# Norms spread through memory, an earlier second chunk, and two reordered steps in an attention and expert kernel

## The chip, the cores and the metric

The kernel runs on one core of one Trainium2 chip. Its engines are TensorE (PE; its weight loads are shown apart as PEld), VectorE (DVE), ScalarE (ACT), GpSimd (POOL) and SyncE (SP), which here only issues transfers. The metric is device time in microseconds (us) for one execution. Three runs of the kernel before took 1643.99, 1644.94 and 1645.40 us.

## The reference, cut to what matters

Four images `x[4, 32, 128, 128]` pass through a channel attention and then through a token layer. Of the first layer:

```
xs = x.reshape(B, C, h, R, w, R).transpose(0, 1, 3, 5, 2, 4).reshape(B, C * R * R, h, w)   # R = 2
q = xs.reshape(B, C * R * R, hw)                     # 128 channels, 64 x 64 = 4096 positions
energy = einsum('bci,bcj->bij', q, q)                # positions against positions
d = sqrt(diagonal(energy, axis1=1, axis2=2))
attn = softmax(energy / (d[:, :, None] * d[:, None, :]), axis=-1)
out = gamma * einsum('bcj,bij->bci', q, attn).reshape(B, C * R * R, h, w) + xs
```

So each position's vector of 128 channels is divided by its own norm `d` before the products. The energy is symmetric, and so are its exponentials; only the row sums make the softmax.

The second layer reads each image as 4096 tokens of 128 values (32 channels of 128 rows each, a row being a token; 32 groups of 128 tokens): a layer norm and a linear attention without softmax (`K^T V`, 8 heads), added to the tokens; then a layer norm, a router over 8 experts, the best two of them with weights that add to one, the experts' products, and the weighted sum added to the tokens. All is float32.

## The kernel before, in words

**Attention.** An image's 4096 positions are cut into 8 chunks of 512, read in four pairs (`kc` 0 to 3). For each chunk the kernel holds `qT` (positions on partitions) and `qn` (channels on partitions, divided by the norm). `attend` walks the lower triangle: for row `i` and tile `jc <= i` it takes four steps `j`. A step emits a product `pe` of `qn` with `qn` (L609), its exponential on ACT with the row sum, `pr` (L612), and, through `after`, things due some steps later: the product `values` into the one bank `po` (L497) two steps later, and for tiles off the diagonal a DVE transpose of `pr` into `F` (L421). When a row is done ACT empties `po` into `o` (L502). Once four steps of a tile are in `F`, SP stores it to memory (L530) and loads it back with its groups swapped (L545), and `transposed_share` multiplies it with `qT` (`pg`, L433) for the mirrored tile; the diagonal has `diagonal_share` (L453).

**Pacing.** The order on PE, DVE, ACT and SP is the order in which the program emits (`manual_schedule`); POOL is pinned where needed. `clock` counts the steps' work: a step adds 8 units (less on the diagonal), a share 4. A share is emitted by `step_share` when its due value, 57 units after its loads, is reached. The side work (preparing chunks, loading weights, the second layer) is written as generators. A table `timed` gives each a window in per cent of the image and a number of moves; a move advances it twice, once before a step and once after. The second layer's parts move every 10 units.

**Preparing a pair of chunks.** `prep` loads `xa` (`load_quarters`, L308), turns it by DVE to `qT` (`turn_quarters`, L316), squares and sums it (L295, L296), and raises the sums to the power -1/2 on POOL (L164), into `rn`, one value per position with positions on partitions. `qn` needs these values along the free axis. So DVE widens `rn` (`wide`, L388), PE transposes `wide` in four pieces into the bank `pnorm` (L399), and DVE multiplies the rows with it (L372). `prep_first` treats image 0's first pair in another way: it scales `qT` by `rn` (L338) and PE transposes the result (`ptn`, L344). At the program's start `prep_first` and the second pair's `prep` are advanced by hand, before the loop. `xa` lies in the pool `xin` with one buffer.

**Second layer.** `close_rows` divides and adds. `attention_rows(u)` takes eight groups of 128 tokens: three times a product `pat` (L855), whose sum `add_rows` puts into the tokens `T`; then eight statistics (`batch_stats`, L962), the router's first sums (`router_rows`), and `close_stats`, six small DVE operations after which POOL makes `rsf`, `nbf` and `nbo`. `normalise` (L696) on ACT uses these. Several `u` run staggered.

What the walk through a row emits in one step, before:

```
after(2, partial(values, pr[:, c0:], t, c0, CH))
...
turn_tick()
clock[0] += 2 * (CH - c0) // P
step_share()
yield
```

Of the kernel before, what the change touches and what calls it, by code (L numbers as in the profile page):

```python
# [22 lines left out]
def kernel(  # L23
# [258 lines left out]
    def chunks_of(b, kc, st):  # L282
        qT = qpool.tile([P, 2, NJ, P], F32, tag="qT", name=f"qT_{b}_{kc}")
        st.setdefault("qT", {})[2 * kc] = qT[:, 0]
        st["qT"][2 * kc + 1] = qT[:, 1]
        return qT
# [12 lines left out]
        rows = st["T"][:, ts(kc, 8), :]  # L299
        return rows.rearrange("p k (w r) -> p k w r", r=2)  # L300

    def load_quarters(b, kc, queues=(nc.sync, nc.sync)):

        xa = xin.tile([P, 2, 2, 2, HW2, 2], F32, tag="xx", name=f"xa_{b}_{kc}")
        halves = x[b].rearrange("c (s g) w -> c s (g w)", s=2)
        for a in (0, 2, 1, 3):
            first_row = 16 * kc + 4 * a
            queues[a // 2].dma_start(  # L308
                xa[ts(a, S)].rearrange("p s k r w e -> p s (k r w e)"),
                halves[:, :, first_row * W : (first_row + 4) * W],  # L310
            )
        return xa

    def turn_quarters(s, xa, qT):
        for k in range(2):
            nc.vector.transpose(  # L316
                qT[:, s, 2 * k : 2 * k + 2, :].rearrange("p h (e r c) -> p r (h e) c", e=2, r=2),
                xa[:, s, k].rearrange("p r (h t) e -> p (r h) e t", h=2),
            )

    def prep_first(st):

        b, kc = 0, 0
        st["T"] = big1.tile([P, KT, D], F32, tag="T", name="T_0")
        xa = load_quarters(b, kc, (nc.sync, nc.scalar))
        qT = chunks_of(b, kc, st)
        yield
        ss = stat.tile([P, 2 * NJ], F32, tag="ss", name=f"ss_{b}_{kc}")
        rn = stat.tile([P, 2 * NJ, 1], F32, tag="rn", name=f"rn_{b}_{kc}")
        for s in range(2):  # L330
            turn_quarters(s, xa, qT)
            squares(b, kc, s, qT, ss)
            pow_neg_half(rn[:, ts(s, NJ), 0], ss[:, ts(s, NJ)])
        keep_running(40, ps_g, "pg")
        scaled = []
        for s in range(2):
            qs = work.tile([P, NJ, P], F32, tag="qs", name=f"qs_{b}_{kc}_{s}", bufs=2)
            nc.vector.tensor_tensor(qs, qT[:, s], rn[:, ts(s, NJ)].to_broadcast([P, NJ, P]), ALU.mult)  # L338
            scaled.append(qs)
        for s, qs in enumerate(scaled):  # L340
            qn = channels(b, kc, s, st)
            pt, done = hold(f"ptn_{b}_{kc}_{s}", lambda p, qn=qn: nc.scalar.activation(qn, p, AF.Copy))  # L342
            for j in range(NJ):
                nc.tensor.transpose(pt[:, ts(j, P)], qs[:, j, :], ident)  # L344
            done()
            yield

    def prep(b, kc, st):

        ahead = 2 if b == 0 and kc == 1 else 5
        xa = load_quarters(b, kc)
# [3 lines left out]
        for _ in range(ahead):  # L357
            yield
        qT = chunks_of(b, kc, st)
        for s in range(2):  # L360
# [17 lines left out]
        rn = stat.tile([P, 2 * NJ, 1], F32, tag="rn", name=f"rn_{b}_{kc}")  # L378
        for s in range(2):
            squares(b, kc, s, qT, ss)  # L380
            if s == 1:
                pow_neg_half(rn[:, :, 0], ss)
            yield
        for _ in range(ahead - 2):
            yield
        wide = work.tile([P, NJ, 2, 64], F32, tag="qs", name=f"wide_{b}_{kc}", bufs=2)
        for s in range(2):
            nc.vector.tensor_copy(wide[:, :, s], rn[:, ts(s, NJ)].to_broadcast([P, NJ, 64]))  # L388
        yield
        if b:  # L390
            yield

        def scale_all(bank):
            for s in range(2):
                scale(s, bank, lambda ap: ap.rearrange("p (j a t) -> p a j t", a=4, t=S))

        bank, done = hold(f"pnorm_{b}_{kc}", scale_all)
        for j in range(NJ):
            nc.tensor.transpose(bank[:, ts(j, P)], wide[:, j].rearrange("p s c -> p (s c)"), ident)  # L399
        yield  # L400
        done()
        yield
# [7 lines left out]

    BELOW = {1: 0, 2: 1, 3: 3}

    def after(ticks, f):
        queued.append((tick[0] + ticks, f))

    def turn_tick():

        due = [f for at, f in queued if at <= tick[0]]
        queued[:] = [q for q in queued if q[0] > tick[0]]
        for f in due:  # L420
            f()  # L421

    def in_order(ap):
        return ap.rearrange("p (a j c) -> p j a c", a=4, c=S)
# [49 lines left out]
    def attend(b, st):  # L474
# [11 lines left out]
        for i in range(NCH):  # L486
# [94 lines left out]
            for jc in order:  # L581
# [21 lines left out]
                for j in range(NJ):  # L603
# [10 lines left out]
                    own.append(pr)  # L614
                    if ending and jc == order[-1] and j == NJ - 1:
                        st["exps"] = True
                    after(2, partial(values, pr[:, c0:], t, c0, CH))
                    if jc < i and not both:
                        after(1, partial(nc.vector.transpose, Fb[:, :, :, j, :], pr))
                        if j == NJ - 1:  # L620
# [33 lines left out]
    def layer1(b, st):  # L654
# [288 lines left out]
        def attention_rows(u):  # L943

            if u < 3:
                fetch_blocks(u + 1)
            yield
            for g in (2 * u, 2 * u + 1):
                keep[g] = work.tile([P, CH], F32, tag="grp", name=f"xnT_{b}_{g}", bufs=2)
                nc.vector.transpose(keep[g], keep["blocks", u][:, ts(g % 2, 4), :].rearrange("p k d -> p (k d)"))  # L950
                yield
            yield
            la = stat.tile([P, 8, 2 * E], F32, tag="la", name=f"la_{b}_{u}")
            for j0 in range(0, 8, 3):
# [12 lines left out]
            close_stats("f", 8 * u, 8, bs)  # L967
            next(logits)
            yield
            nc.sync.dma_start(t2[:, ts(u, 8)], T[:, ts(u, 8), :])  # L970
            yield
            for g in (2 * u, 2 * u + 1):
                normalise(range(4 * g, 4 * g + 4), rsf, nbo)
                if g % 2:
                    for _ in logits:
                        pass
                yield
                yield
            if u % 2:
                for _ in route(u // 2):  # L980
# [4 lines that stand above are left out]
                yield from sorted_experts(u // 2)  # L985
# [510 lines left out]
    for b in range(B):  # L1496

        if b == 0:
# [80 lines left out]
```

## Time and profile before

One execution was profiled.

| | |
|---|---|
| median of three runs | 1644.94 us |
| the profiled execution | 1638.94 us |
| its span | 1637.1 us |
| granted PE clock, mean | 0.996 |
| instructions | 20938 |
| memory read, written | 166.90 MB, 182.09 MB |
| `pr` exponentials on ACT (L612) | 576, mean 560 ns |
| `po` products (L497) | 1152 records, mean 559 ns |
| `pe` products (L609, 128x512 of two chunks) | 896 records, mean 596 ns |
| `pg` products (L433) | 880 records, mean 593 ns |
| `F` transposes (L421) | 440, mean 700 ns |
| POOL's power for a chunk pair (L164, 128x8) | 15, mean 1660 ns |

How to read it: an f32 product shows as two records on PE. The records' durations overlap, because products are pipelined; the distance between starts tells what a product costs. The profile counts as idle what lies between the end of one record and the start of the next, and names who released the waiting instruction. A granted clock below 1 means that PE ran at a part of its speed in that stretch. Along the chain of waits PE has 84% of the span, with L497 25%, L609 24% and L433 21%.

### The profile page before, as it was taken

To read this page: it belongs to the slowest core of one execution; us is meant where nothing else is said; L and a number is where in the kernel's file an instruction comes from. 1 tells how busy PE (TensorE), PEld (TensorE's weight loads), DVE (VectorE), ACT (ScalarE), POOL (GpSimd) and SP (SyncE) were. 2 spreads that over 40 slices of the span, in tenths; PEclk is the share of its full clock that TensorE was granted. 3 is DMA by queue.
4 is the path that set the end of the run, shared out by engine and by line. 5 is a ranking of instruction groups with operands and counts; after the bars stand their busy time and mean duration, and the time that the engine had idled before them with its cause. 6 is when DMAs were issued, how large, how long until landed. Compare 5 with 4: busy or idle time off the path is not lost.

```text
span 1637.1 us, 20938 instructions
## 1 busy us (share of the span) xinstructions
PE 1598.4 (98%) x5075; PEld 832.8 (51%) x5075; DVE 942.7 (58%) x2383; ACT 877.2 (54%) x2779; POOL 593.8 (36%) x565
## 2 busy tenths in 40 slices
PE   8999999999999999999999999999999999999887
PEld 5444444455554455555554445555554445555633
DVE  5444353468487454449468545447758644344786
ACT  3555445456465544546555554556646554555386
POOL 1000000001024442446545553156555653437166
PEclk9999999999999999999999999999999999999999
DMA  4555656675759798997898889798798989886001
GB/s 139 199 193 174 202 179 213 236 231 179 171 206 269 238 230 248 255 263 206 208 221 270 263 214 277 216 281 222 203 212 256 298 238 257 252 254 192 15 14 39
DMA packets 364728, 345.18 MB, mean 211 GB/s; under 512 B 157504, under 2 KB 291136, under 8 KB 350272
## 3 DMA queue, kind: packets, MB, share of 16 engines
q1 hardware_dynamic: 330144, 304.33, 62.1%
q0 software_dynamic: 26624, 25.58, 7.7%
q10 hardware_dynamic: 7840, 13.93, 2.9%
q8 instruction: 43, 0.70, 0.2%
q14 instruction: 77, 0.63, 0.1%
HBM read 166.90 MB, written 182.09 MB: 213 GB/s over the span
## 4 chain that ended last, share of the span: by engine, by line
PE 84%; DVE 6%; DMA 4%; ACT 2%; issue 1%; POOL 1%; SPq 1%; ACTq 0%; DVEq 0%; POOLq 0%
PE po L497 25%; PE pe L609 24%; PE pg L433 21%; PE py L1371 3%; PE pg L453 2%; DMA F<-blocks 2%; PE pys L1180 2%; PE pys L1130 2%; PE pgram L725 2%; PE pat L855 1%; SPq L545 1%; DMA below<-F 1%; PE pys L1137 1%; ACT xn L696 1%; ACT pr L612 1%
## 5 line engine op out<-in xcount | busy, mean ns | idle before, releaser
L612 ACT ACTIVATE pr<-pe 128x512 f32<-128x512 f32 (+1 forms) x576 | 322.4, 560 | 614.5 <-PE pe L609 592.1
L497 PE MATMUL po<-pr,qT 128*128 128x512 f32 (+3 forms) x1152 | 549.8, 559 | 4.2 <-ACT o L502 3.5
L609 PE MATMUL pe<-qn,qn 128*128 128x512 f32 x896 | 460.4, 596 | 4.7 <-ACT pr L612 4.7
L433 PE MATMUL pg<-F,qT 128*128 128x512 f32 x880 | 450.4, 593 | 4.6 <-DMA F<-blocks 4.6
L421 DVE STREAM_TRANSPOSE F<-pr 128x512 f32<-128x512 f32 x440 | 305.1, 700 | 167.5 <-ACT pr L612 160.1
L497 PEld LDWEIGHTS po<-pr,qT 128*128 128x128 f32 x1152 | 215.6, 191 | 251.5 <-issue 219.4
L1245 POOL DMA_INDIRECT acc<-ys,place x128 | 202.1, 1579 | 210.4 <-ACT pr L612 135.0
L438 ACT ACTIVATE junk<-F 128x512 bf16<-128x512 f32 x440 | 273.1, 621 | 5.1 <-DMA F<-blocks 5.1
L433 PEld LDWEIGHTS pg<-F,qT 128*128 128x128 f32 x880 | 166.7, 190 | 199.5 <-issue 176.2
L1066 POOL DMA_INDIRECT xs<-xn,place x192 | 185.7, 967 | 176.3 <-ACT pr L612 109.8
L609 PEld LDWEIGHTS pe<-qn,qn 128*128 128x128 f32 x896 | 158.0, 191 | 131.4 <-issue 119.2
L442 DVE TENSOR_TENSOR o<-o,pg 128x512 f32<-128x512 f32 x110 | 75.2, 683 | 244.6 <-PE pg L433 244.4
L164 POOL TENSOR_TENSOR rn<-ss,neg_half 128x8 f32<-128x8 f32 (+1 forms) x17 | 27.2, 1603 | 321.0 <-DVE ss L296 320.9
L612 ACT ACTIVATION_READ_ACCUMULATOR pr<-pe 128x1 f32 x576 | 111.8, 194 | 0.0
L609 PE MATMUL pe<-qn 128*128 128x512 f32 (+3 forms) x256 | 91.5, 440 | 0.7 <-ACT qn L342 0.7
L1245 POOL DMA_INDIRECT yb<-ys,place x64 | 61.0, 953 | 77.8 <-DMA ys<-results 47.5
L438 ACT ACTIVATION_READ_ACCUMULATOR junk<-F 128x1 f32 x440 | 84.6, 192 | 0.0
L1112 DVE TENSOR_TENSOR results<-pys,xn 128x256 f32<-128x256 f32 (+1 forms) x60 | 24.9, 416 | 83.5 <-ACT xn L1106 70.4
L164 POOL TENSOR_TENSOR rsa<-dm_a,neg_half 128x8 f32<-128x8 f32 x16 | 28.9, 1807 | 104.7 <-DVE sv_a L688 104.6
L696 ACT ACTIVATE xn<-T,nbo,rsf 128x128 f32<-128x128 f32 x128 | 54.1, 495 | 20.7 <-POOL nbo L692 20.7
L1371 PE MATMUL py<-ew_sb,xn 128*128 128x512 f32 x128 | 60.2, 610 | 5.0 <-ACT tmp L1327 3.9
L164 POOL TENSOR_TENSOR rsf<-dm_f,neg_half 128x8 f32<-128x8 f32 (+1 forms) x15 | 26.3, 1751 | 105.2 <-DVE sv_f L688 105.2
(221 smaller groups left out, 1508.0 us busy)
## 6 DMA issues: line engine op xcount, KB each, us to landing
blocks<-F SPq DMA_DIRECT2D x110, 1024.0 KB
F<-blocks SPq DMA_DIRECT2D x220, 192.0 KB
F<-blocks SPq DMA_DIRECT2D x220, 128.0 KB
F<-blocks SPq DMA_DIRECT2D x220, 64.0 KB
below<-F SPq DMA_DIRECT2D x31, 384.0 KB
T<-in_x_dram SPq DMA_DIRECT2D x64, 128.0 KB
out_dram<-acc SPq DMA_DIRECT2D x128, 64.0 KB
xa<-in_x_dram SPq DMA_DIRECT2D x62, 128.0 KB
```

The source lines that it names most:

```text
L164: pinned(nc.gpsimd.tensor_tensor(dst, src, neg_half.to_broadcast(list(src.shape)), ALU.pow))
L421: f()
L433: nc.tensor.matmul(pg.rearrange("p (a f) -> p a f", a=4), st["qT"][i][:, ib, :], G[:, :, ib], start=(ib == 0), stop=(ib == NJ - 1),)
L438: nc.scalar.activation(junk, G[:, :, ib], AF.Copy, accum_out=st["sums"][:, NJ * i + ib, jc : jc + 1])
L442: nc.vector.tensor_tensor(st["o"][jc], st["o"][jc], pg, ALU.add)
L497: nc.tensor.matmul(row["po"][:, lo:hi], qT[blk // NJ][:, blk % NJ, :], w, start=start, stop=(row["left"] == 0))
L609: nc.tensor.matmul(pe[:, c0:], qn[jc][:, ts(j, P)], qn[i][:, c0:], start=True, stop=True)
L612: nc.scalar.activation(pr[:, c0:], pe[:, c0:], AF.Exp, accum_out=sums[:, t, i : i + 1]).ins
L696: nc.scalar.activation(xn[:, k, :D], T[:, k, :], AF.Identity, scale=rs[:, k, :], bias=nb[:, k, :])
L1066: inst = nc.gpsimd.indirect_dma_start(xs[h], offset(place[:, i, k : k + 1]), xn[:, k, :], None)
L1245: inst = nc.gpsimd.indirect_dma_start(to, None, ys, offset(place[:, i, k : k + 1]), compute_op=op)
L1371: nc.tensor.matmul(bank, xn[:, k, :D], ew_sb[:, 4 * h : 4 * h + 4, :], start=True, stop=True)
```

## The change

It has four parts.

1. **Norms.** For every pair except image 0's first two, POOL writes the power into one of two fixed tiles `norms` (128x32, of which 8 columns are used, the rest set to 1 at the start). DVE transposes the tile in blocks of 32, SP stores it (16 KB) to a memory tile, and two SP loads bring it back, each row repeated over 64 partitions, into `spread_...`. There are five yields after the store and five after the loads; then `scale` multiplies with that tile. `wide`, its two copies, the four transposes and the bank `pnorm` go, except for image 0's second pair.
2. **Image 0's start.** The second pair is loaded into another pool (`work`, tag `wide`) right after the first. Its four turns stand between the first pair's steps, whose order is now written by hand; its squares follow at once. Its generator then has 8 moves from 1.3 to 5.5% instead of 10 from 0.5%. The order by hand begins before `prep_first`'s work instead of after it.
3. **Statistics.** In `attention_rows` each sum is followed by the statistics of its two or three groups, and `close_stats` follows the last at once; the router's first sums come two yields after it.
4. **Share first.** At the third step of a row's first tile, the `values` that are due are emitted behind the share.

The tile `weight` has one buffer instead of two. The diff, cut to its core:

```diff
-    def load_quarters(b, kc, queues=(nc.sync, nc.sync)):
-        xa = xin.tile([P, 2, 2, 2, HW2, 2], F32, tag="xx", name=f"xa_{b}_{kc}")
+    def load_quarters(b, kc, queues=(nc.sync, nc.sync), place=(xin, "xx")):
+        xa = place[0].tile([P, 2, 2, 2, HW2, 2], F32, tag=place[1], name=f"xa_{b}_{kc}")
...
+    def turn_quarter(s, k, xa, qT):
+        nc.vector.transpose(
+            qT[:, s, 2 * k : 2 * k + 2, :].rearrange("p h (e r c) -> p r (h e) c", e=2, r=2),
+            xa[:, s, k].rearrange("p r (h t) e -> p (r h) e t", h=2),
+        )
...
+    norms = [const.tile([P, S], F32, tag=f"norm{n}", name=f"norm_{n}") for n in range(2)]
+    for norm in norms:
+        nc.gpsimd.memset(norm, 1.0)
...
     def prep_first(st):
...
+        scaled = []
+        keep_running(40, ps_g, "pg")
+        summed(0, rows_squared(0))
+        sq = rows_squared(1)
+        st["turns"].pop(0)()
+        scale_rows(0)
+        summed(1, sq)
+        st["turns"].pop(0)()
+        st["turns"].pop(0)()
+        scale_rows(1)
+        st["turns"].pop(0)()
...
+    def spread_over_rows(norm, nm, tag, spread, gap):
+        turned = stat.tile([P, S], F32, tag="turned", name=f"turned_{nm}", bufs=1)
+        nc.vector.transpose(turned, norm)
+        yield
+        kept = dram.tile([P, S], F32, tag="norms", name=f"norms_{nm}", bufs=3)
+        nc.sync.dma_start(kept, turned)
+        for _ in range(gap):
+            yield
+        wide = work.tile([P, CH], F32, tag=tag, name=f"spread_{nm}", bufs=2)
+        for s in range(2):
+            nc.sync.dma_start(
+                wide[ts(s, 64)].rearrange("p (a f) -> p a f", a=4),
+                kept.rearrange("(a q) t -> a (q t)", q=S)[:, ts(s, P)].partition_broadcast(64),
+            )
+        spread.append(wide)
+        for _ in range(gap):
+            yield
...
     def prep(b, kc, st):
...
+        if not on_chip:
+            yield from idle(1)
+            yield
+            spread = []
+            yield from spread_over_rows(norm, f"{b}_{kc}", "qs", spread, 5)
+            for s in range(2):
+                scale(s, spread[0], lambda ap: ap.rearrange("p (a j t) -> p a j t", a=4, t=S))
+            yield
+            return
...
-    def turn_tick():
-        due = [f for at, f in queued if at <= tick[0]]
+    def turn_tick(starts=False):
+        due = [q for q in queued if q[0] <= tick[0]]
         queued[:] = [q for q in queued if q[0] > tick[0]]
-        for f in due:
-            f()
+        for _, f, can_wait in due:
+            if not (starts and can_wait):
+                f()
+        return [f for _, f, can_wait in due if starts and can_wait]
...
-                    after(2, partial(values, pr[:, c0:], t, c0, CH))
+                    after(2, partial(values, pr[:, c0:], t, c0, CH), True)
...
-                    turn_tick()
+                    left = turn_tick(jc == order[0] and j == 2)
                     clock[0] += 2 * (CH - c0) // P
                     step_share()
+                    for f in left:
+                        f()
                     yield
...
-        weight = stat.tile([P, 2, KT, 1], F32, tag="weight", name=f"weight_{b}")
+        weight = stat.tile([P, 2, KT, 1], F32, tag="weight", name=f"weight_{b}", bufs=1)
...
                 attend_rows(u, j0, pa)
                 yield
                 done()
-            bs, stats = batch_stats("f", 8 * u, 8)
-            for j in range(8):
-                stats[j]()
-                if j == 3:
-                    yield
-                    yield
+                for f in stats[j0 : j0 + 3]:
+                    f()
+            close_stats("f", 8 * u, 8, bs)
+            yield
+            yield
             logits = router_rows(nc.vector, 8 * u, 8, la)
-            close_stats("f", 8 * u, 8, bs)
             next(logits)
-            yield
             nc.sync.dma_start(t2[:, ts(u, 8)], T[:, ts(u, 8), :])
+            yield
             yield
...
-    next(first)
-    load_weights()
+    ordered = ExitStack()
     next(first)
     next(second)
+    load_weights()
+    ordered.enter_context(tc.manual_schedule(engines=ENGINES))
+    next(second)
+    next(first)
     load_tokens(states[0]["T"][:, 0:8, :], 0, 0, 8)
-
-    ordered = ExitStack()
-    ordered.enter_context(tc.manual_schedule(engines=ENGINES))
-    timed = [(first, 0, 1, 2), (second, 0.5, 5.5, 10)]
+    next(second)
+    next(second)
+    timed = [(first, 0, 1, 2), (second, 1.3, 5.5, 8)]
```

In `prep_first`, `rows_squared(s)` is the two turns and the square of half `s`, `summed` its sum and the power, `scale_rows` its scaling (as before, into tag `grp`).

More of the change, by code (lines that the diff above doesn't have):

```diff
@@ L312, in load_quarters @@
         return xa
+    def turn_quarter(s, k, xa, qT):
[3 more added lines that the diff above has]
+        )
     def turn_quarters(s, xa, qT):
         for k in range(2):
[L316 to L319, printed above, removed]
+            turn_quarter(s, k, xa, qT)
+    norms = [const.tile([P, S], F32, tag=f"norm{n}", name=f"norm_{n}") for n in range(2)]
+    for norm in norms:
+        nc.gpsimd.memset(norm, 1.0)
     def prep_first(st):
@@ L328, in prep_first, with rows_squared, summed, scale_rows @@
         ss = stat.tile([P, 2 * NJ], F32, tag="ss", name=f"ss_{b}_{kc}")
-        rn = stat.tile([P, 2 * NJ, 1], F32, tag="rn", name=f"rn_{b}_{kc}")
-        for s in range(2):
+        rn = norms[0][:, : 2 * NJ][:, :, None]
+        def rows_squared(s):
             turn_quarters(s, xa, qT)
-            squares(b, kc, s, qT, ss)
+            sq = work.tile([P, NJ, P], F32, tag="qs", name=f"sq_{b}_{kc}_{s}", bufs=2)
+            nc.vector.tensor_tensor(sq, qT[:, s], qT[:, s], ALU.mult)
+            return sq
+        def summed(s, sq):
+            nc.vector.tensor_reduce(ss[:, ts(s, NJ)], sq, AX.X, ALU.add)
             pow_neg_half(rn[:, ts(s, NJ), 0], ss[:, ts(s, NJ)])
[L334 to L337, printed above, removed]
+        def scale_rows(s):
+            qs = work.tile([P, NJ, P], F32, tag="grp", name=f"qs_{b}_{kc}_{s}", bufs=2)
             nc.vector.tensor_tensor(qs, qT[:, s], rn[:, ts(s, NJ)].to_broadcast([P, NJ, P]), ALU.mult)
             scaled.append(qs)
+        scaled = []
[9 more added lines that the diff above has]
+        st["turns"].pop(0)()
         for s, qs in enumerate(scaled):
@@ L346, in prep_first @@
             yield
-    def prep(b, kc, st):
-        ahead = 2 if b == 0 and kc == 1 else 5
-        xa = load_quarters(b, kc)
+    def spread_over_rows(norm, nm, tag, spread, gap):
[15 more added lines that the diff above has]
+            yield
+    def prep(b, kc, st):
+        soon = b == 0 and kc == 1
+        ahead = 2 if soon else 5
+        if soon:
+            xa = load_quarters(b, kc, place=(work, "wide"))
+            yield
+        else:
+            xa = load_quarters(b, kc)
         if b == 0:
@@ L356, in prep @@
             xx = rows_of_image(b, kc, st)
-        for _ in range(ahead):
+        qT = chunks_of(b, kc, st)
+        if soon:
+            st["turns"] = [partial(turn_quarter, s, k, xa, qT) for s in range(2) for k in range(2)]
             yield
-        qT = chunks_of(b, kc, st)
-        for s in range(2):
+        for _ in range(0 if soon else ahead):
+            yield
+        for s in range(0 if soon else 2):
             turn_quarters(s, xa, qT)
@@ L377, in scale @@
                 )
-        rn = stat.tile([P, 2 * NJ, 1], F32, tag="rn", name=f"rn_{b}_{kc}")
+        on_chip = b == 0 and kc == 1
+        norm = norms[kc % 2]
         for s in range(2):
@@ L381, in prep @@
             if s == 1:
-                pow_neg_half(rn[:, :, 0], ss)
+                pow_neg_half(norm[:, : 2 * NJ], ss)
             yield
+        if not on_chip:
[7 more added lines that the diff above has]
+            return
+        rn = norm[:, : 2 * NJ][:, :, None]
         for _ in range(ahead - 2):
@@ L389, in prep @@
         yield
-        if b:
-            yield
+        yield
         def scale_all(bank):
@@ L411, with after @@
     BELOW = {1: 0, 2: 1, 3: 3}
-    def after(ticks, f):
-        queued.append((tick[0] + ticks, f))
-    def turn_tick():
-        due = [f for at, f in queued if at <= tick[0]]
+    def after(ticks, f, can_wait=False):
+        queued.append((tick[0] + ticks, f, can_wait))
+    def turn_tick(starts=False):
+        due = [q for q in queued if q[0] <= tick[0]]
         queued[:] = [q for q in queued if q[0] > tick[0]]
-        for f in due:
-            f()
+        for _, f, can_wait in due:
+            if not (starts and can_wait):
+                f()
+        return [f for _, f, can_wait in due if starts and can_wait]
     def in_order(ap):
@@ L953, in attention_rows @@
             la = stat.tile([P, 8, 2 * E], F32, tag="la", name=f"la_{b}_{u}")
+            bs, stats = batch_stats("f", 8 * u, 8)
             for j0 in range(0, 8, 3):
@@ L959, in attention_rows @@
                 done()
-            bs, stats = batch_stats("f", 8 * u, 8)
-            for j in range(8):
-                stats[j]()
-                if j == 3:
-                    yield
-                    yield
+                for f in stats[j0 : j0 + 3]:
+                    f()
+            close_stats("f", 8 * u, 8, bs)
+            yield
+            yield
             logits = router_rows(nc.vector, 8 * u, 8, la)
-            close_stats("f", 8 * u, 8, bs)
             next(logits)
+            nc.sync.dma_start(t2[:, ts(u, 8)], T[:, ts(u, 8), :])
             yield
-            nc.sync.dma_start(t2[:, ts(u, 8)], T[:, ts(u, 8), :])
             yield
```

## The prediction

> **What bounds the kernel now.** I read the page's first part, then TensorE's waits, then the timeline at each wait.
>
> ```profile
> PE 1598.4 (98%) x5075; PEld 832.8 (51%) x5075; DVE 942.7 (58%) x2383; ACT 877.2 (54%) x2779; POOL 593.8 (36%) x565
> ```
>
> TensorE (PE) is busy for all but 38.7 us of 1637.1. Every product taken off it, and every wait of its own, is time; work of the other engines counts only where it makes PE wait. Its waits (total, times, longest):
>
> ```profile
> PE pe L609 <- ACT pr L612: 4.7, 3, 1.6
> PE pg L433 <- DMA F<-blocks: 4.6, 3, 2.3
> PE po L497 <- ACT o L502: 3.5, 14, 0.5
> PE pnorm L399 <- DVE wide L388: 2.5, 2, 2.2
> PE ptn L344 <- DVE qs L338: 2.2, 1, 2.2
> ```
>
> Four of these five are touched; only the waits for F's transfer are not aimed at. In the timeline an f32 product is a pair (x2), and a 128x512 pair is followed by the next one 0.86 us later; that start-to-start time is the price used below, since the durations overlap.
>
> **Norms through DRAM.** Of 15 chunks that use the four `pnorm` transposes (60 in the tile's view), 14 lose them; only image 0's chunk 1 keeps them. The chain of waits, read in time order, has one such group:
>
> ```profile
> 60.16 0.22 PE po L497 x2
> 60.38 0.44 PE pnorm L399 x4
> 60.82 0.86 PE pe L609 x2
> ```
>
> It stands in a gapless PE: 14 x 0.44 = **6.2 us** gone. In exchange each chunk gets a 128x32 DVE transpose in place of two copies of 286 ns (the 128x256 transposes take 413, so no more than before), and SP gets three issues: a 16 KB store and two 128 KB loads, together 42 issues and 3.8 MB beside 345 MB. The scaling multiplies read SBUF where they read PSUM; 64x512 from PSUM took 686 ns, the 128x512 square from SBUF 667, so no change. They come some eight yields later; the tightest, chunk 3 of a later image (17 moves from 38 to 62%, scaled at the 12th: 53.5%), is still ahead of row 6, which starts at about 56%.
>
> A rule speaks against this part: the Trainium skill, "DMA: Bandwidth & Descriptors", section "Anatomy of one DMA", gives a DMA a fixed cost of about 2 us, mostly the receipt from the memory written. Two legs would be 4 us per chunk, 56 us if PE waited for them. This trace agrees on the size: `below` was stored from SP at 17.43 (0.35) and its loads went out at 19.78, 2.0 us later. But after the store the generator yields five times, and again after the loads; two yields are one move and a move is at least one step of 2.58 us (po starts 477.70, 480.28, 482.85), so each leg has 2.5 steps, over 6 us. I take 0. The other end: SP stands in order, and behind the store (which waits for DVE, which waits for POOL's power) stand the loads of F. These have room: issued by 35.69, first used at 46.18, so 10.5 us less the 2 us landing. Cover gone, each chunk costs what the F wait at 849 us cost: 2.3 idle and about 1.3 of slow clock, 3.6.
>
> **Image 0's start.** Now:
>
> ```profile
> 19.70 0.38 PE L497 MATMUL po<-pr,qT 128*128 128x128 f32 x2
> 22.32 1.07 PE L399 MATMUL pnorm<-ident,wide 128*128 128x128 f32 x4 [2.23 <-DVE wide L388]
> 23.18 1.92 PE L609 MATMUL pe<-qn,qn 128*128 128x512 f32 x2
> 24.89 1.49 PE L497 MATMUL po<-pr,qT 128*128 128x512 f32 x2
> 26.22 1.02 PE L609 MATMUL pe<-qn,qn 128*128 128x512 f32 x2
> ```
>
> PE could have gone on at 19.92 (19.70 and 0.22) and stood until 22.32: 2.40 lost. Then the group took 0.86 to the next start instead of 0.44, the next pair 1.71 instead of 0.86, the next 1.33 instead of 0.86: 1.74 more, at this clock (columns: stretch, length, busy of PE, PEld, DVE, ACT, POOL, then granted clock):
>
> ```profile
> 20.00:22.00 2.00, 0.09 (x1) 0.00 (x0) 0.87 (x4) 1.08 (x3) 1.63 (x1) 1.00 0.33 86
> 22.00:24.00 2.00, 1.68 (x5) 1.21 (x6) 1.45 (x4) 0.00 (x0) 0.00 (x0) 0.60 0.22 62
> 24.00:26.00 2.00, 2.00 (x4) 0.91 (x3) 1.94 (x4) 0.69 (x2) 0.00 (x0) 0.54 0.00 0
> ```
>
> The clock fell to about half after 2.4 us of standing. The Trainium skill ("TensorE: Matmul & The Clock Gate", Part 1) puts the fall after an idle window of about 3.4 us; by that rule this gap costs its 2.40 alone, by the row 4.14. I take the row.
>
> What replaces it, with this trace's durations: DVE starts at 5.44 when the first chunk lands. Two turns 0.73, square 0.57, sum 0.58: 7.32, where the first sum ended at 8.05 before. POOL's power (0.15 to start, 1.35) ends at 8.82. Meanwhile two turns, a square (8.62) and one turn of the second chunk (0.37, 8.99); scale 0.70: 9.69 instead of 10.28. PE starts **0.59 earlier**. This needs the second chunk in SBUF at 8.62: its four loads stand on SP right after the first chunk's, so they go out from 2.1 to 4.6 (0.62 each), and the first chunk landed 2.9 after its last issue: about 7.5. Later landing costs us for us. The token loads on SP now stand behind them and are first read about 20 us in: free. They competed with the first chunk's load before as the new ones do now.
> DVE goes on: second sum to 10.27, power to at most 11.8, scale 12.5, last turn 12.9, two squares and sums 2.6: 15.5, power 1.64: 17.2, `wide` 0.50: 17.7. PE needs it at 19.33. So no wait: 4.14 + 0.59 = **4.7 us**. F's small transposes now stand behind the squares on DVE, from 15.5 instead of 14.03; their store went out at 17.43, so nothing is late. The gap before the first transposes (8.15 to 9.7) may still slow the clock for 12 to 16 us as now (0.54, 0.60); if not, up to 1.7 more. I take 0.
>
> **Share first.** At a row's third step PE waits for ACT to empty the one `po` bank:
>
> ```profile
> 97.18 1.02 PE L609 MATMUL pe<-qn,qn 128*128 128x512 f32 x2
> 98.39 1.12 PE L497 MATMUL po<-pr,qT 128*128 128x512 f32 x2 [0.18 <-ACT o L502]
> 99.35 1.02 PE L433 MATMUL pg<-F,qT 128*128 128x512 f32 x2
> ```
>
> The idle shown is 0.18; by starts it is 98.39 - 97.18 - 0.86 = 0.35, and 0.10 more until the next: 0.45. Running the share's pair (0.86) first covers that. By the pacing code (a step adds 8 units, less on the diagonal, a share 4) in 23 of 32 rows no share falls on step two and one on step three, so there is something to put first (image 0's row 2 has none and keeps its wait). Looking for these gaps in windows of 20 us gives 17: 14 like this and 3 with 0.50 shown, 0.55 by starts (each image's first row). 14 x 0.45 + 3 x 0.55 = **7.9 us**; some records lack a releaser, which is why the waits say 14. Nothing is added: the same pairs change places. The share's F was there in all but three cases.
>
> **Statistics with each sum.**
>
> ```profile
> 486.29 0.81 PE L453 MATMUL pg<-F,qT 128*128 128x384 f32 x2
> 488.62 1.13 PE L609 MATMUL pe<-qn,qn 128*128 128x512 f32 x2 [1.52 <-ACT pr L612]
> 489.58 1.02 PE L497 MATMUL po<-pr,qT 128*128 128x512 f32 x2
> 486.35 1.65 ACT L696 ACTIVATE xn<-T,nbo,rsf 128x128 f32<-128x128 f32 x4 [3.79 <-POOL nbo L692]
> ```
>
> ACT stands 3.79 for a bias that POOL makes from statistics; the exponentials queue behind. PE loses 488.62 - 486.29 - 0.65, and 0.10: 1.78; at 875 and 1260 likewise 1.83 and 1.82: 5.4. The last sum ended at 479.74 and the closing six operations at about 484.0, two yields and 4.3 us later. With the statistics beside their sums the six earlier ones (0.21 each) delay the last sum by at most 1.3 on a full DVE; two more 0.43, closing 0.8: 482.0, 2.0 earlier, where 1.7 to 1.8 is needed. That is close, so of 5.4 I take **4.5**. The normalisation stays at the same yield, so nothing else moves.
>
> **Sum.** 6.2 + 4.7 + 7.9 + 4.5 = 23.3. The profiled execution took 1638.94 (span 1637.1 and 1.8 around it): 1615.6. The median of the runs lies 6.0 above that execution; I forecast for it 1644.94 - 23.3 = **1621.6**.
>
> **Rivals.**
> - Partial (0.22): the statistics gain nothing because DVE is full there (5.4 idle remain), or the share put first waits for its own F, or the second chunk lands late. One failing: 1626 to 1630; two: up to 1634. For it: DVE is busy 18.5 of 20 us there. Against: three independent places must fail.
> - F's waits go too (0.08): the timing shifts and the two stalls at 849 and 1232 (about 3.6 and 2.5 us) vanish: 1615.5.
> - Slower (0.05): SP blocks behind the norms' stores while POOL's power stands behind gathers, and F comes late at every chunk of images 1 to 3: 12 x 3.6 = 43, so 1665. It decides only from a block of over 8 us; SP's own longest wait for a blocks store is 6.8, so against it.
> - The norms' part hides nothing (0.03): another engine bounds once PE is lighter. No other passes 58%, so 1640 to 1648.
>
> **How the numbers follow.** Forecast 0.62. The range of 8 in 10 runs from 1613.5 (F's waits gone, first gap warm) to 1634 (two parts fail). What this kernel's measurement can tell from no change is 0.2%, 3.3 us: faster 0.92, same 0.03, slower 0.05.
>
> **What would show it.** After: 4 `pnorm` transposes instead of 60; no wait of PE between 12 and 36 us and a full clock from 18 on; `po <- ACT o` down to one or two times; `pe <- ACT pr` under 1 us in all; PE still 98 to 99% busy. A wait of `pg` for F above 8 us in total, or one of DVE for the spread norms, would make it wrong.

## The result and the profile after

The changed kernel takes 1634.29 us (median of 7 runs, 1631.79 to 1640.89), the kernel before beside it 1643.99 (1642.64 to 1647.26): a ratio of 0.9936, 95% interval 0.9922 to 0.9951. It is faster, by 9.7 us where 23.3 were forecast; the forecast's range ended at 1634.0. Two later measurements, beside the kernel before on two other chips, gave 0.994 (0.9917 to 0.9963) and 0.9926 (0.990 to 0.9953).

The profiled execution took 1636.16 (span 1634.4). The page's first part:

```profile
PE 1592.9 (97%) x5019; PEld 830.1 (51%) x5019; DVE 940.0 (58%) x2369; ACT 877.2 (54%) x2779; POOL 596.2 (36%) x567
```

PE has 56 instructions fewer (14 groups of four) and 5.5 us less work. Its idle time, span less busy, did not fall: 41.5 us, where it was 38.7. So the removed waits have been replaced. PE's waits now (total, times, longest):

```profile
PE pg L495 <- DMA F<-blocks: 5.4, 3, 2.8
PE ptd L585 <- remote: 5.1, 1, 5.1
PE py L1434 <- ACT tmp L1390: 3.9, 4, 2.5
PE pg L495 <- DVE F L482: 2.7, 3, 1.2
PE pe L671 <- ACT pr L674: 2.1, 1, 2.1
...
PE pys L1193 <- ACT xn L1169: 1.5, 1, 1.5
PE pe L671 <- ACT pr_back L652: 1.4, 1, 1.4
```

The waits that the change aimed at are gone: `po` for ACT's `o` is left once (0.2 us), the start waits for nothing at `pnorm`. In the timeline of PE, image 0's start from 18 us on is gapless:

```profile
18.16 0.38 PE L559 MATMUL po<-pr,qT 128*128 128x128 f32 x2
18.38 0.60 PE L459 MATMUL pnorm<-ident,wide 128*128 128x128 f32 x4
18.82 1.02 PE L671 MATMUL pe<-qn,qn 128*128 128x512 f32 x2
19.68 1.04 PE L559 MATMUL po<-pr,qT 128*128 128x512 f32 x2
20.55 1.02 PE L671 MATMUL pe<-qn,qn 128*128 128x512 f32 x2
```

What had started at 26.22 starts at 20.55: 5.67 earlier. New are waits for F's transpose on DVE, for ACT in image 3, and a 5.1 us wait whose releaser the trace can't name. Two of the forecast's signs came out otherwise: PE is 97% busy, not 98 to 99, and `pe <- ACT pr` is 2.1 us, not under 1.

To see where time is won and given back, I set a milestone of each row, the start of ACT's eviction `o` at the row's end (8 rows an image), in the changed kernel against the first trace of the kernel before, in us:

```
image row    before   changed  difference
0     1       36.25     30.58       -5.67
0     7      360.02    351.06       -8.96
1     5      572.04    558.23      -13.81
1     6      649.05    638.23      -10.82
2     5      958.80    942.07      -16.73
2     6     1035.81   1021.11      -14.70
3     4     1285.41   1266.74      -18.67
3     7     1530.28   1526.07       -4.21
```

Up to row 4 of image 3 the parts bring 18.7 us. Of what they bring, 3.0 and 2.0 are lost between rows 5 and 6 of images 1 and 2, and 14.5 after row 4 of image 3. Two questions: what takes the first, and does the second belong to the change?

### The profile page after: what moved, and what is told of

The parts are those of the page before. It is cut to its first block, busy times and chain, and to the rows that moved or that the text cites. A ratio compares the mean times of both kernels' runs of the same rounds, so it can differ in the third digit from the quotient of the medians.

```text
span 1634.4 us, 20871 instructions
## 1 busy us (share of the span) xinstructions
PE 1592.9 (97%) x5019; PEld 830.1 (51%) x5019; DVE 940.0 (58%) x2369; ACT 877.2 (54%) x2779; POOL 596.2 (36%) x567
## 4 chain that ended last, share of the span: by engine, by line
PE 89%; DVE 3%; DMA 3%; SPq 2%; ACT 1%; issue 1%; another core or an unknown queue 1%; POOL 0%; ACTq 0%; DVEq 0%
PE po L559 26%; PE pe L671 26%; PE pg L495 22%; PE py L1434 3%; PE pg L515 2%; PE pys L1193 2%; PE pgram L789 2%; PE pat L919 1%; PE pys L1243 1%; SPq L607 1%; PE pys L1200 1%; DMA F<-blocks 1%; SPq L1215 1%; DMA ys<-results 0%
## 5 line engine op out<-in xcount | busy, mean ns | idle before, releaser
L164 POOL TENSOR_TENSOR norm<-ss,neg_half 128x8 f32<-128x8 f32 (+1 forms) x17 | 27.0, 1586 | 311.9 <-DVE ss L296 304.4
L671 PEld LDWEIGHTS pe<-qn 128*128 128x128 f32 x256 | 45.1, 191 | 38.1 <-issue 33.7
```

Source lines behind the costliest of these rows:

```text
L164: pinned(nc.gpsimd.tensor_tensor(dst, src, neg_half.to_broadcast(list(src.shape)), ALU.pow))
L671: nc.tensor.matmul(pe[:, c0:], qn[jc][:, ts(j, P)], qn[i][:, c0:], start=True, stop=True)
```

## The experiments

**One part undone, and one part alone.** Four kernels are the changed one with one part put back, four the kernel before with one part put in. The smallest edit of each kind:

```diff
 (share undone)
-                    left = turn_tick(jc == order[0] and j == 2)
+                    left = turn_tick()
 (norms undone: every chunk spread on TensorE)
-        on_chip = b == 0 and kc == 1
-        norm = norms[kc % 2]
+        on_chip = True
+        norm = norms[1] if b == 0 and kc == 1 else stat.tile([P, 2 * NJ], F32, tag="rn", ...)
```

The start is put back by the old `prep_first`, the old order of the first calls and the window (second, 0.5, 5.5, 10); the statistics by the old loop after all the sums. The kernels with one part alone put the other three back.

Norms undone:

> The changed kernel with the norms again spread on TensorE (14 groups of four transposes back, no store and loads of norms); the other three parts stay. Changed kernel: median 1634.3 us. Theory 'the norms' extra transfers give the gain back': by the milestones the first rows of image 3 were 18.7 us early and 14.5 of it was lost in its last three rows; if the 42 extra transfers cause that, this kernel gets 14 us back less the 6.2 us of transposes, about 1626, and its row 7 of image 3 ends as early as its row 4 does. Theory 'floor' (the end of image 3 waits for work that is not TensorE's, so whatever is gained before is absorbed there): within 3 us of the changed kernel, 1634 to 1637. Theory 'parts add up, the loss is elsewhere': 6.2 more, 1640.5.

Share undone:

> The changed kernel with the row's values again before the share in the first tiles; the other three parts stay. Parts add up: 7.9 us slower than the changed kernel (1634.3), so 1642, with the 17 waits of the row's product for ACT's eviction back. Floor theory: at most 3 us slower, 1634 to 1637, although the waits are back. Norms' transfers theory: as parts add up, 1642, with the loss of some 14 us in image 3's last rows still there.

Statistics undone:

> The changed kernel with the statistics again after all the sums; the other three parts stay. Parts add up: 4.5 to 5.4 us slower than the changed kernel, 1639 to 1639.7, with three waits of 1.5 us for exponentials back. Floor theory: at most 2 us slower. By the milestones of the two profiles only about 1.35 us a time of the 1.8 stayed (2.2 gained and about 0.7 given back within ten exponentials), so 4 us would be no surprise.

Start undone:

> The changed kernel with the start of image 0 as before (second chunk turned after the first's steps); the other three parts stay. The two profiles show 5.67 us gained by image 0's second row. Parts add up: 4.7 to 5.7 us slower than the changed kernel, 1639 to 1640. Floor theory: at most 2 us slower, since 1500 us lie between this part and the end of image 3.

Measured, in this order, against the kernel before: 0.995 (0.993 to 0.9969), 0.995 (0.9932 to 0.9968), 0.9951 (0.9931 to 0.997), 0.9956 (0.9942 to 0.9971). That looked like the floor. It was not safe to say, because the chip of these four runs was another one: the kernel before took 1634.5 there, not 1644, and the changed kernel was not run on it. And their milestones are even from row 4 to row 7 of image 3 (-0.1 to +0.5 us): the loss of 14.5 was in none of them, though three of the four have the norms through DRAM. So the changed kernel and the kernel before were run again, with two parts alone.

> The changed kernel once more, unchanged, beside the kernel before. The four runs with one part undone stood at 0.9950, 0.9950, 0.9951 and 0.9956 of the kernel before on their chip, where the changed kernel was at 0.9936 in the first measurement. Theory 'each part is worth something, but about half': the changed kernel stands at 0.9930 to 0.9940, so undoing one part costs 2 to 4 us each. Theory 'floor': it stands at 0.995, as all four do. Theory 'the loss in image 3's last rows belongs to one execution': the milestones of rows 4 to 7 of image 3 stay even, as they did in the four, and the loss of 14 us is not seen; if it belongs to the kernel, it is there again.

> The kernel before once more, for a second trace of it on the chip of the run above. If the first trace of it was a lucky execution (1638.94 beside a median of 1644), this trace shows more waits than the first, above all for the transfers of F and in image 3; if the two traces agree within 2 us at every row, the spread lies in the changed kernel.

> The kernel before with nothing but the share put first in the rows' first tiles. By the forecast's sum 7.9 us faster than the kernel before (ratio 0.9952). Half-size theory (the 0.45 us a row is shown by the profile, but part of it comes back as TensorE arrives earlier at F's transfer): 3 to 4 us faster, 0.998. Floor theory: up to the whole gain of 8 us on its own, since on its own it meets no floor.

> The kernel before with nothing but the norms spread through DRAM. By the forecast's sum 6.2 us faster (ratio 0.9962). Half-size theory: 2 to 3 us faster, 0.9985. If the extra transfers delay F: as slow as before or slower, with longer waits for F.

The changed kernel stood at 0.994, as the half-size theory had it; 0.995 lies inside its interval, so the floor was not excluded by this alone. The share alone gave 0.9961 (0.9946 to 0.9975): 6.4 us of the forecast 7.9, and that value is inside. **The norms alone gave 1.0011 (0.9993 to 1.0029): no gain, where 6.2 us were forecast.** The second trace of the kernel before was 6.8 us worse in image 3 from row 4 to row 7 than the first, so comparing with the first had made the changed kernel look worse there than it was. The first trace also stands apart by its time: on these chips no other of 75 executions of that kernel took less than 1641.34 us, while on the chip of the four runs they took 1632.49 to 1641.68, and 1638.94 lies among those. Its chip is not on record.

**Where the norms give it back.** In the kernel with the norms alone the rows lose 3.2 and 2.5 us between rows 5 and 6 of images 1 and 2. The waits of all engines from 540 to 640 us in the changed kernel begin so:

```profile
ACT pr L674 <- PE pe L671: 44.9, 30, 2.7
POOL xs L1129 <- ACT pr L674: 32.2, 13, 4.4
DVE xn L1221 <- DMA xn<-xs: 18.4, 8, 5.8
```

The third line, DVE waiting 18.4 us for the loads of sorted tokens, has no counterpart before. The same line stands in every trace so far of a kernel with the norms through DRAM (18 to 23 us in image 1) and in none without. These loads stand on SP. SP's own waits in the changed kernel have this line:

```profile
SPq L308 <- DVE qn L422: 19.0, 2, 10.2
```

Twice in the kernel, once in image 1 and once in image 2, the load of a chunk (L308, `xa`) waits for the scaling of the chunk before (`qn`). The timeline of SP and of DVE's scaling there:

```profile
532.70 2.66 SPq L607 DMA_DIRECT2D F<-blocks  x6
545.68 2.54 SPq L308 DMA_DIRECT2D xa<-in_x_dram  x4
548.27 0.58 SPq L592 DMA_DIRECT2D blocks<-F  x1
```

```profile
542.89 2.76 DVE L422 TENSOR_TENSOR qn<-xx,spread 64x512 f32<-64x512 f32 x4
```

SP is done with F at 535.36 and stands until 545.68; the scaling ends at 545.65. In the kernel before, SP sent the same load right behind its predecessor:

```profile
547.41 2.67 SPq L545 DMA_DIRECT2D F<-blocks  x6
550.18 2.50 SPq L308 DMA_DIRECT2D xa<-in_x_dram  x4
```

The reason is in the code: the pool `xin` has one buffer, used for `xa` and `xx` in turn, and the scaling is the last to read it. The window of a later image's chunk 3 ends its scaling at 53.5% of the image, by the forecast's own count; the next image's chunk 0 begins at 52%. On TensorE the scaling came at about 48%, and SP did not wait (in the kernel with the norms undone it ends at 533.1 and the load goes out at 538.70). The block store behind it is 10 us late, then the tokens' loads, then DVE. On PE this shows as six short waits, 2.1 us in all, between rows 5 and 6 of image 1 (changed kernel, 558 to 638 us; the rest of what is lost there shows no wait):

```profile
PE pg L495 <- DVE F L482: 0.9, 1, 0.9
PE pys L1243 <- DVE results L1227: 0.4, 2, 0.3
PE pys L1243 <- issue: 0.4, 2, 0.3
PE pg L495 <- DMA F<-blocks: 0.4, 1, 0.4
```

One number of the schedule tests it:

```diff
-            timed.append((prep(b + 1, 0, nxt), 52, 78, 17))
+            timed.append((prep(b + 1, 0, nxt), 57 if b else 52, 79 if b else 78, 17))
```

> The changed kernel with one number moved: in images 1 and 2 the next image's first chunk begins at 57 per cent of the image instead of 52 (and ends at 79 instead of 78). Theory 'one buffer': xin has one buffer, so the load of that chunk stands on SP until the chunk before is scaled, and through DRAM that is at 55 per cent, not at 49; in every kernel with the norms through DRAM SP waits for that scaling twice (15 to 19 us together, longest about 10), the block stores and the loads of the sorted tokens behind it come 10 us late, and DVE waits for these loads 18 to 21 us in image 1 and again in image 2. It expects both SP waits gone or under 1 us, DVE's waits for the sorted tokens under 3 us an image, and 4 to 6 us less time than the changed kernel (two places, 2 to 3 us each). Theory 'the transfers themselves load the memory': same time as the changed kernel within 1 us, DVE's waits still there.

The mark beside it, the changed kernel again, to compare on one chip:

> The changed kernel once more on the chip of the others of this call: the mark against which the run above is read. 0.994 of the kernel before by the two measurements so far.

The last two single parts went along:

> The kernel before with nothing but the new start of image 0. By the forecast's sum 4.7 us faster (ratio 0.9971); by the milestones of the changed kernel 5.7 us by image 0's second row (0.9965). If a gain of the start is absorbed later: under 2 us (0.9988 or more).

> The kernel before with nothing but the statistics taken with each sum. By the forecast's sum 4.5 us faster (ratio 0.9973). By the milestones about 1.4 us a time stay: 4 us (0.9975). If the gain is absorbed in the sorting right after: under 2 us (0.9988 or more).

With the later window both SP waits are gone, and DVE's waits for these loads with them. Its SP timeline:

```profile
553.99 2.67 SPq L607 DMA_DIRECT2D F<-blocks  x6
556.76 0.37 SPq L616 DMA_DIRECT2D below<-F  x1
557.17 2.56 SPq L308 DMA_DIRECT2D xa<-in_x_dram  x4
```

The load goes out right behind its predecessor, and between rows 5 and 6 of images 1 and 2 PE has no wait over 0.15 us left. There this trace gains 0.9 us in both images (0.44 for a group of transposes and 0.44 for a share put first), where its mark lost 2.9 and 1.2: 3.8 and 2.1 us had back. So what makes these two losses is shown. In the time of the whole it is not resolved: 0.9902 (0.9876 to 0.9928) against 0.9926 (0.990 to 0.9953) on the same chip, medians 1634.55 and 1636.85. The theory that the transfers load the memory falls: they are all still there.

The start alone: 0.997 (0.9949 to 0.999), 4.9 us. The statistics alone: 0.998 (0.9964 to 0.9995), 3.3 us. In the trace of the statistics alone the three waits of 1.5 us are gone, and each place gains 1.8 us by the exponentials around it, 5.4 together, as forecast before the deduction. But two waits of PE for F's transfer, at 847 and 1231 us, one after each of the first two gains, are longer:

```profile
PE pg L480 <- DMA F<-blocks: 6.2, 2, 3.2
```

At these two places the traces of the kernel before have 2.3 and 1.9 us, and 1.3 and 1.4.

**Image 3.** On the slower chips (1644 us and more for the kernel before) every trace so far loses between row 4 and row 7 of image 3 against the first trace of the kernel before. Without norms through DRAM in that image: the kernel before 6.8, start alone 7.4, statistics alone 7.9, share alone 8.3. With them: norms alone 10.9, the changed kernel 14.5, 12.5 and 12.1, later window 15.6. On the faster chip (four traces): none. Such a loss looks like this on ACT (changed kernel, second trace):

```profile
1290.83 0.62 ACT L500 ACTIVATE junk<-F 128x512 bf16<-128x512 f32 x1
1291.35 0.19 ACT L500 ACTIVATION_READ_ACCUMULATOR junk<-F 128x1 f32 x1
1296.56 0.60 ACT L674 ACTIVATE pr<-pe 128x512 f32<-128x512 f32 x1 [5.02 <-PE pe L671]
1297.06 0.20 ACT L674 ACTIVATION_READ_ACCUMULATOR pr<-pe 128x1 f32 x1
1297.15 0.62 ACT L500 ACTIVATE junk<-F 128x512 bf16<-128x512 f32 x1
1297.67 0.19 ACT L500 ACTIVATION_READ_ACCUMULATOR junk<-F 128x1 f32 x1
1302.26 0.60 ACT L674 ACTIVATE pr<-pe 128x512 f32<-128x512 f32 x1 [4.40 <-remote]
```

ACT waits 5.0 and then 4.4 us for products that the trace has PE start at 1291.76 and 1294.33. The trace's semaphore events (not in a view of the page) show why it names no releaser: PE's signals of completion come late and together, five of them between 1302.19 and 1302.40, after 5.7 us with none. POOL issues a scatter of the experts' tokens every 1.27 us there (median), and in row 7 gathers at the same rate.

One thing makes these signals a weak witness. The traces with the loss lack part of their semaphore events: of PE's 1540 or so completions they hold 1346 to 1378, and none is missing before 400 us. The five traces without the loss, the first of the kernel before and the four of the faster chip, hold all but one at most. So the loss may belong to the chip or to the recording of the execution; no run here separates the two.

Three kernels and a mark asked whether norms, early arrival or these transfers are the cause:

```diff
 (norms of image 3 on TensorE, with the later window)
-        on_chip = b == 0 and kc == 1
+        on_chip = b == 0 and kc == 1 or b == B - 1 and kc >= 2
 (transfers set apart, with the later window)
-                if b < B - 2 and n % 4 == 3:
+                if b < B - 1 and n % 4 == 3:
...
-                        if n % 2:
-                            yield
-                            yield
-                            due()
+                        yield
+                        yield
+                        due()
```

> The changed kernel with the later window once more, as the mark of this call: 0.990 of the kernel before; in image 3 from row 4 to row 7 about 15 us more than the first trace of the kernel before on a chip of the slower kind, none on one of the faster kind.

> The later window, and in image 3 alone the norms of its last two chunks again on TensorE (two groups of transposes, 0.9 us, back). Theory 'the norms' transfers cost in image 3': the loss from row 4 to row 7 of image 3 falls from about 15 to 7 or 8 us, and the time is 6 us under the run with the later window. Theory 'earlier arrival or the chip': the loss stays at 13 to 16 us and the time is within 1.5 us of that run.

> The changed kernel without any norms through DRAM, once more. It arrives at image 3 some 14 us before the kernel before, but has no transfers of norms. Theory 'the norms' transfers cost in image 3': on a chip of the slower kind it loses 7 to 8 us from row 4 to row 7, as the kernels without these transfers do, and stands at 0.992 or less. Theory 'earlier arrival': it loses 11 us or more.

> The later window, with the indirect transfers of image 2's experts during image 3 set apart: a pause after every fourth scatter, as in the other images, and one gather a step instead of two. Gathers that no longer fit before image 3 ends run after it, so the whole is expected 20 us slower or more; to be read is image 3 from row 4 to row 7 alone. Theory 'these transfers hold up the signals of TensorE': the loss there falls below 5 us on a chip of the slower kind, and no burst of late signals is left. Theory 'something else of the chip': it stays at 12 us or more.

Lost from row 4 to row 7: the mark 17.8 us, norms of image 3 on TensorE 7.6, no norms through DRAM 11.7, transfers set apart **0.0**, and there no burst of late signals (four or more within 0.3 us after 1.2 us without one) was left, where the other three have two each. (The burst is no sure sign: the kernel with the norms alone lost 10.9 us without one.) PE's longest waits from row 4 to row 7, for the mark (1265 to 1528 us):

```profile
PE ptd L585 <- ACT gd L575: 6.7, 1, 6.7
PE pe L671 <- ACT pr_back L652: 2.6, 1, 2.6
PE pe L671 <- ACT pr L674: 2.2, 1, 2.2
PE pe L671 <- issue: 0.8, 1, 0.8
```

and all of them with the transfers set apart (1258 to 1503 us), where nothing is left that is ACT's:

```profile
PE pbd L835 <- DVE rdx L813: 1.9, 1, 1.9
PE pys L1200 <- DMA xn<-xs: 0.4, 1, 0.4
```

PE does the same 195 records of experts' products in both stretches (8 of `ptx` are missing in the second), so PE's work has not simply left it. What moves within it makes 6.4 us gained up to row 6 and 6.4 lost after. But only 32 of the 64 gathers are issued there. That trace lacks signals as the others do (it holds 1379), so lost signals alone do not make the loss. So the loss needs these transfers as they stood; whether their density or their number counts is not told apart. They are not enough for it: the first trace of the kernel before and those of the faster chip have them as dense and lose nothing. As a whole that kernel is slower, 1.0066 (1.0051 to 1.0081): the gathers that are left run after image 3, and PE stands 41.5 us there. Whether the norms add to the loss stays open: six traces on the slower chips with norms through DRAM in image 3 lie between 10.9 and 17.8, six without between 6.8 and 11.7, but the ratios of the mark and of the kernel with image 3's last norms on TensorE are the same, 0.9929 (0.9913 to 0.9946) and 0.993 (0.9905 to 0.9954), with medians of 1634.68 and 1630.62. The 7.6 fits the theory of the norms' transfers, the 11.7 that of the earlier arrival. Without any norms through DRAM the changed kernel stood at 0.9954 (0.9938 to 0.997).

The last two tried to have this loss back without the rest at the end. The pace of image 2's experts is a third entry of `steady`, 6 or 8 instead of 10.

> The later window, one gather a step instead of two during image 3, and image 2's experts stepped every 6 units of work instead of 10 there so that the gathers are done in time. Theory 'the density of the gathers makes the loss': from row 6 to row 7 of image 3, where the gathers run and where 13 us were lost in the run with the later window, at most 3 us are lost against the first trace of the kernel before; the 4 us from row 4 to 5, where the scatters run, stay. Time 6 to 10 us under the run with the later window, 0.986 to 0.989 of the kernel before. Theory 'density as such': with a faster step the scatters come closer together and lose more than 4 us there, so the time is no better than 0.990.

> The later window, a pause after every fourth scatter in image 3 as in the other images, gathers two a step as they were, and image 2's experts stepped every 8 units instead of 10. Theory 'the gathers make the loss': from row 6 to row 7 still some 10 us lost, from row 4 to 5 under 2; time 0.990 to 0.993. Theory 'the scatters make it': nothing lost in either, 0.983 to 0.987.

Gathers apart at pace 6: 1.0087 (1.0069 to 1.0105). From row 6 to 7 PE waits 1.9 us where the mark waits 9.8, so most of the gathers' loss is gone (that it gains 6.1 us there is work moved away: none of the mark's 61 records of experts' products are left). But the faster step draws the experts' work and scatters together, as the second theory had it: from row 4 to 5 25.3 us are lost. PE's waits there are 15.1 us, one of 12.6 among them; the rest goes with work moved forward, 64 records of experts' products where the mark has 14. Pauses at pace 8: 0.9918 (0.9897 to 0.9938), 1631.85 us; from row 4 to 5 it gains 1.2 where the mark lost 4.3, from row 5 to 6 it loses 4.0 where the mark lost 0.6, and from row 6 to 7 it loses 8.9 where the mark lost 12.9: 11.6 in all for 17.8. The scatters' part is gone, and the larger one stays with the gathers, as the first theory had it. So the later window, with or without these, stands at 0.9902 to 0.993 of the kernel before, the changed kernel at 0.9926 to 0.994: better by the middle of the intervals, not outside them.

## Why the forecast was wrong

**Norms through DRAM: this step failed.** The 14 groups are gone and each gave its 0.44 us (the steps show in the milestones). The failing sentence is "I take 0" for the exchange. I had asked whether SP would stand behind the norms' stores, and compared the scaling's 53.5% with the row that needs it, at 56%. I did not ask who else waits for the scaling: the one buffer of `xin`, wanted at 52% by a load that stands on the same in-order queue as everything else. SP's stop of 10.2 us is over the 8 us from which the forecast itself had said that a stop would decide. Set against the 0.9 us that each place should have gained, it costs 2.1 to 3.9 us a place, 4.6 to 6.8 us in each of the three traces of the changed kernel; a cover gone had been put at 3.6. In all, the part measures +1.8 us alone (-1.2 to +4.8) where the sum had -6.2; of these 8.0 us the two places hold 6.5 in that kernel's trace, and the rest stays open. With the later window the part does pay: on one chip 0.9929 with it and 0.9954 without any norms through DRAM, some 4 us, though the two intervals overlap. The fixed cost of a DMA that the Trainium skill gives ("DMA: Bandwidth & Descriptors", section "Anatomy of one DMA") is told there for transfers issued by GpSimd; these go out from SP, where this trace's 2.0 us stood for it. Its two legs were hidden nearly as forecast: DVE waits for the spread loads three times, 2.6 us in all, which the forecast had named as a sign against it. That is not what cost PE its time: such waits are still there with the later window (2.3 us).

**Image 0's start: right in size, not in its parts.** Forecast 4.7 (4.14 for the second gap and 0.59 for an earlier first scale), alone 4.9 (1.6 to 8.4). The 4.14 came: in each of the 14 traces with the new start 4.1 us are gained between row 0 and row 1 of image 0. The 0.59 did not: the first transposes stand at 10.29, where they were at 10.32. DVE started 0.25 later (5.69 for 5.44), and its eight steps before the scale took 3.9 us where I had counted 3.55.

The 5.67 of the changed kernel's trace has 1.5 us more, from the clock, and that is luck. There the gap before the first transposes was 1.27 us (it had been 2.18), and the clock stayed full; in the trace of the start alone the gap was 2.26, and it fell. One stretch of each, first the changed kernel:

```profile
12.00:14.00 2.00, 2.00 (x9) 1.02 (x8) 1.97 (x4) 1.20 (x3) 0.00 (x0) 1.00 0.02 6
12.00:14.00 2.00, 2.00 (x6) 0.98 (x7) 1.79 (x4) 0.42 (x1) 0.14 (x1) 0.56 0.10 24
```

(columns: stretch, length, busy of PE, PEld, DVE, ACT, POOL, granted clock, DMA share, GB/s.) Of the 14 traces with the new start 7 kept the full clock there, of the 6 with the old start one.

**Share first: right.** 6.4 us alone (4.1 to 8.9) for 7.9, one wait for ACT's `o` left of 17, in image 0's row 2 as said.

**Statistics with each sum: the mechanism right, the net too large.** PE's three waits are gone, 5.4 us by the exponentials. 3.3 remain (0.8 to 5.9; the forecast's 4.5 is inside). The waits for F's transfer, which I had left untouched, are longer by 0.8 to 1.7 us each in that trace; that PE's earlier arrival makes them so is likely, but no run tests it.

The four parts alone sum to -6.4 + 1.8 - 4.9 - 3.3 = -12.8 us; the whole measured 9.9 to 12.2 by its three ratios. So the parts add up within their intervals, and no floor is needed. Of the 10.5 us between the forecast's sum and this one, 8.0 are the norms, 1.5 the share and 1.2 the statistics. Of the 14.5 us that the first pair of traces showed in image 3, about half is not the change: the second trace of the kernel before loses 6.8 there too. Against that trace the changed kernel's loss is 5 to 8 us larger, and how much of that is the norms stays open.

Of the rivals, "partial" was the nearest, with the wrong part failing; the slower one had the right place, SP's queue, and the wrong blocker.

## What to carry to other kernels

A value that is made later holds its inputs longer: beside the consumer's due time, look up when the buffers that it reads are wanted again, and which queue the waiting load stands on. Where one part of a change measures nothing alone, compare milestones row by row with a kernel without it, and look for a wait that is new on another engine. Take two traces of the kernel before, on the chip of the comparison, before a difference near the end is put down to the change, and see whether both hold all their events.

## What the runs showed of the hardware

- In image 3, with indirect transfers issued by POOL every 1.27 us, the slower chips' traces show up to 9.2 us without a completion signal of PE, and ACT waiting 5.0 and 4.4 us for products whose records on PE start 4.8 and 7.9 us before; with the transfers set apart the loss of 7 to 18 us was nil. A full DMA does not explain it: in the changed kernel the DMA engines were 80% busy at 1290 to 1300 us, but 33% at 1490 to 1500 and 13% at 1500 to 1510, where PE waited 5.1 us. All traces with the loss lack an eighth of PE's signals, so the recording is not ruled out as a cause. Why a chip does so was not found.
- The same kernel took 1634.5 us on one chip and 1644 to 1648 on others (medians). The four traces from the faster chip, all of other kernels, have no such loss; that it makes up the difference of 10 to 13 us is not shown.
- Over the 20 traces (from 5 us to 1540 us), PE's gaps of 1.1 to 1.86 us (64) were never followed by half clock within 3.5 us, those of 1.87 to 3.46 us (68) were in 41 cases, and the 10 of 3.59 us and more always. That the clock "fell to about half after 2.4 us of standing", as the forecast read it, is thus a chance at that length, not a rule.
